# Graph attention on one Trainium2 core: exact float32r passes move from the last projection to the first, and five blocks of W2 are read from DRAM each round

## The chip, the cores and the metric

The kernel runs on one core of a Trainium2 chip. The metric is the device time of one execution in microseconds, the median of several runs. The output must agree with a float32 reference. Engines are named as the profile names them: PE is TensorE (PEld its weight loads), DVE is VectorE, ACT is ScalarE, POOL is GpSimd, SP is SyncE, whose queue issues nearly all DMAs here.

## The reference, cut to what matters

There are 64 graphs of 256 nodes with 512 features. Each goes through a normalisation, a GAT of two attention layers with a residual, a second normalisation, and a third attention layer with a residual.

```python
def gat_layer(x, mask, W, a_src, a_dst, bias, concat):
    xl = (x @ W).reshape(B, N, H, F)
    asrc = jnp.einsum('bnhf,hf->bnh', xl, a_src)
    adst = jnp.einsum('bnhf,hf->bnh', xl, a_dst)
    e = leaky_relu(asrc[:, :, None, :] + adst[:, None, :, :], 0.2)
    attn = softmax(where(mask[..., None], e, NEG_INF), axis=1)
    out = jnp.einsum('bsdh,bshf->bdhf', attn, xl)
    ...
h = maximum(layernorm(x), 0)
h1 = elu(gat_layer(h, mask, W1, ..., concat=True))     # 512 -> 4 heads x 256
x = x + gat_layer(h1, mask, W2, ..., concat=False)     # 1024 -> 1 head x 512
h = maximum(layernorm(x), 0)
x = x + attention(h, adj, W_proj, W_att, b_att)        # 512 -> 8 heads x 64, relu
```

So a graph has three projections: W1 (256x512 by 512x1024), W2 (256x1024 by 1024x512) and W_proj (256x512 by 512x512). Each weight is widened by "logit" columns, W times the attention vectors, so that the scores come out of the same product.

## The kernel before

**Tiles.** A graph's 256 nodes are two tiles (t = 0, 1) of 128 partitions. `Graph` (line 293) has one small method for each step of a graph; `Weights` (line 667) has the steps that prepare weights.

**Three ways of projecting.** The first and second projections are plain float32, as Strassen-Winograd products (`Product`, line 46): a 2x2 split of rows and inner dimension against inner dimension and columns gives seven half-size products instead of eight. Steps `p1` to `p7` are matmuls (line 62), `q1`, `q6`, `q7` copies of a partial sum out of PSUM on ScalarE (line 68), and `q2`, `q3`, `c22`, `q4` write the result (`total`, line 262: a sum on VectorE, or a copy on ScalarE). The left side needs four sums on GpSimd (`left`, line 221), the right side four sums of weight blocks once (`right`, line 626). W1 is done as two column halves `m1a` and `m1b` (tiles `w1a_sb`, `w1b_sb`), W2 as `m2` (`w2_sb`, all seven blocks in SBUF).

The last projection is three float32r passes (lines 524 to 563). The operand is split into a high part (`high3`, ScalarE, times `DOWN`), a low rest (`low3`, GpSimd) and a mixed part (`mix3`, VectorE); the weights are split likewise in `wk_sb`. `u3` and `w3` accumulate two passes in one PSUM bank, `v3` does the third in another; `k3` copies the first out with a factor, `d3` subtracts the second. It works in two halves of 4 heads: 264 columns (4 x 64 features and 2 logits a head) per matmul.

**Turning.** A tile is transposed by writing it to DRAM and reading it back in another layout (`away1`/`home1`, `send2`/`take2`, `away3`/`home3`), then by 32x32 transposes on VectorE (`back1`, `back2`, `back3`). The last graph uses TensorE instead.

**Attention.** `exp`, `ship`, `rows` send the exponentials of the scores over DRAM to all partitions, `edges` (`weigh`, line 286) makes the weights on ScalarE and VectorE, `gat` multiplies on TensorE, `out` divides on VectorE.

**Order.** The order of all instructions is written out by hand as text. `head` runs once, `order` once for each round r = 2 to 62, `tail` at the end. An item such as `-2 m2 p3` is step p3 of the second projection of graph r - 2. A round carries five graphs at different stages. Each engine and SP's DMA queue take their instructions strictly in this order; a DMA whose buffer is not free holds up those behind it. Buffers rotate: `kept` has 3, `hk` 5, `ez` 2.

Of the kernel before, what the change touches and what calls it, by code (L numbers as in the profile page):

```python
# [19 lines left out]
P = 128  # L20
# [12 lines left out]
KEPT = 3  # L33

DOWN = 1.0 - 2.0 ** -13
UP = 1.0 + 2.0 ** -12
LIFT = 2.0 ** 12
EVEN = 2.0 ** -80
# [7 lines left out]
class Product:  # L46
# [8 lines left out]
    def __init__(self, nc, ps_sum, ps_mm, work, lhs, rhs, put):  # L55
        self.nc, self.ps_sum, self.ps_mm, self.work, self.lhs, self.rhs, self.put = (
            nc, ps_sum, ps_mm, work, lhs, rhs, put)
        self.nk, self.n = rhs.shape[2], rhs.shape[3]

    def product(self, to, i, first, last):  # L60
        for c in range(self.nk):
            self.nc.tensor.matmul(to[:, :self.n], self.lhs[:, i, c, :], self.rhs[:, i, c, :],  # L62
                                  start=(first and c == 0), stop=(last and c == self.nk - 1),
                                  skip_group_check=True)

    def kept(self):
        s = self.work.tile([P, 264], F32, name="kept", bufs=KEPT)
        self.nc.scalar.activation(s[:, :self.n], self.sum[:, :self.n], AF.Copy)  # L68
        return s
# [48 lines left out]
def short_path(ctx, tc, flags, x, adj, w1, att_src1, att_dst1, b1, w2, att_src2, att_dst2, b2, w_proj, w_att,  # L118
# [47 lines left out]
    L1, L2 = 4, 1  # L166
    w1_sb = [const.tile([P, 7, DC // 2, L1 + Q], F32, name="w1a_sb"),
             const.tile([P, 7, DC // 2, Q], F32, name="w1b_sb")]
    w2_sb = const.tile([P, 7, HC // 2, L2 + Q], F32, name="w2_sb")
    wk_sb = const.tile([P, 3, 2, DC, G * (K3 + 2)], F32R, name="wk_sb")  # L170
# [97 lines left out]
    def put1(i):  # L268
        at, n = (0, L1 + Q) if i == 0 else (L1, Q)

        def put(t, half, pm, add):
            total(xl1[:, t, 2 * i + half, at:at + n], pm[:, :n], add if add is None else add[:, :n])
        return put

    def put2(t, half, pm, add):
        n = L2 + Q
        total(xl2[:, t, half, :n], pm[:, :n], add if add is None else add[:, :n])

# [14 lines left out]
    class Graph:  # L293


        def __init__(self, b):
# [3 lines left out]
            self.hk, self.us, self.ks, self.vs = {}, {}, {}, {}  # L300
# [54 lines left out]
        def products1(self):  # L355
            self.a1 = work.tile([P, 7, DC // 2, P], F32, name="hs", bufs=1)
            self.m1 = [Product(nc, ps_sum, ps_mm, work, self.a1, w1_sb[i], put1(i)) for i in range(2)]

        def square1(self, t):
            return self.a1[:, 4 * t:4 * t + 2].rearrange("p r k m -> p (r k) m")  # L360

        def turn0(self):
            self.products1()
            for t in range(T):
                turn(self.h, self.square1(t), t)
            left(self.a1, DC // 2)
# [14 lines left out]
        def back1(self, t):  # L381
            if self.a1 == 1:
                self.products1()
            back(self.h, self.square1(t), t)

        def left1(self):
            left(self.a1, DC // 2)
# [7 lines left out]
        def exp1(self):  # L395
            self.exs()
            exps(self.w[0], self.ex1, H1, xl1[:, :, 0, :L1], xl1[:, :, 1, :L1])
# [26 lines left out]
        def ez1(self, g, t):  # L424
            ez = self.e["ez", g, t] = work.tile([P, 2 * F1], F32, name="ez")
# [20 lines left out]
        def back2(self, g, t):  # L446
            if not self.a2:
                self.a2 = work.tile([P, 7, HC // 2, P], F32, name="h1s", bufs=1)
                self.m2 = Product(nc, ps_sum, ps_mm, work, self.a2, w2_sb, put2)
# [3 lines left out]
            else:  # L453
# [3 lines left out]
                nc.scalar.activation(a.rearrange("p k q -> p (k q)"), pm, AF.Copy)  # L457

# [61 lines left out]
        def back3(self, t):  # L520
            self.raw = work.tile([P, DC, P], F32, name="raw", bufs=1)
            (back if self.gone else turn)(self.h, self.raw, t)

        def part(self, i, t):
            a = self.hk[i, t] = work.tile([P, DC, P], F32R, name="hk", bufs=5)
            return a

        def high3(self, t):

            nc.scalar.activation(self.part(0, t), self.raw, AF.Copy, scale=DOWN)  # L530

        def low3(self, t):
            nc.gpsimd.tensor_tensor(self.part(1, t), self.raw, self.hk[0, t].bitcast(F32), ALU.subtract)  # L533

        def mix3(self, t):

            nc.vector.scalar_tensor_tensor(self.part(2, t), self.hk[0, t].bitcast(F32), UP, self.raw, ALU.mult, ALU.subtract)

        def uv(self, pm, i, j, half, t, first, last):
            for c in range(DC):  # L540
                nc.tensor.matmul(pm[:, :G * (K3 + 2)], self.hk[i, t][:, c], wk_sb[:, j, half, c],  # L541
                                 start=(first and c == 0), stop=(last and c == DC - 1))

        def u3(self, half, t):
            self.us[half, t] = ps_sum.tile([P, 512], F32, name="sum")
            self.uv(self.us[half, t], 0, 0, half, t, True, False)

        def w3(self, half, t):
            self.uv(self.us[half, t], 1, 1, half, t, False, True)

        def k3(self, half, t):
            s = self.ks[half, t] = work.tile([P, 264], F32, name="kept", bufs=KEPT)
            nc.scalar.activation(s, self.us.pop((half, t))[:, :264], AF.Copy, scale=UP)

        def v3(self, half, t):
            self.vs[half, t] = ps_mm.tile([P, 512], F32, name="pm")
            self.uv(self.vs[half, t], 2, 2, half, t, True, True)

        def d3(self, half, t):
            def heads(s):  # L560
                return s[:, :G * (K3 + 2)].rearrange("p (h k) -> p h k", h=G)
            nc.vector.tensor_tensor(xl3[:, t, half * G:(half + 1) * G, :K3 + 2], heads(self.ks.pop((half, t))),
                                    heads(self.vs.pop((half, t))), ALU.subtract)
# [47 lines left out]

    graphs = [Graph(b) for b in range(B)]
# [6 lines left out]
    def bring(w, src, at, r, by):  # L619

        nk, n = w.shape[2], w.shape[3]
        for half in range(2):
            rows = src[:, at + half * Q:at + (half + 1) * Q].rearrange("(p c) f -> p c f", p=P)
            by[half].dma_start(blocks(w)[r][half][:, :, n - Q:], rows[:, r * nk:(r + 1) * nk])

    def right(w):
        b11, b21, t2, t1, t3, t4, b22 = (w[:, i] for i in range(7))
# [14 lines left out]
    for r in range(2):  # L642
        bring(w1_sb[1], w1, 2 * Q, r, (nc.sync, nc.scalar))
# [5 lines left out]
    for r in range(2):  # L649
        bring(w1_sb[0], w1, 0, r, (nc.sync, nc.scalar))  # L650
    nc.sync.dma_start(b2_sb, rows_of(b2, D2))
    for a, src in zip(att2, (att_src2, att_dst2)):
        nc.sync.dma_start(a, rows_of(src, D2))
    for r in range(2):
        for half in range(2):
            nc.sync.dma_start(blocks(w2_sb)[r][half][:, :, -Q:],
                              w2[r * (HF // 2):(r + 1) * (HF // 2), half * Q:(half + 1) * Q].rearrange("(p c) f -> p c f", p=P))
        if r == 0:
            nc.sync.dma_start(b1_sb, rows_of(b1, HF))
    nc.sync.dma_start(batt_sb, rows_of(b_att, H3))  # L660
    raw3 = work.tile([P, 2, DC, G * (K3 + 2)], F32, name="h1s", bufs=1)
    for half in range(2):
        for c in range(DC):
            nc.sync.dma_start(raw3[:, half, c].rearrange("p (h k) -> p h k", h=G)[:, :, 2:],
                              w_proj[:, half * Q:(half + 1) * Q].rearrange("(p c) (h k) -> p c h k", p=P, h=G)[:, c])

    class Weights:


        def __init__(self):  # L670

            self.dots = sorted(((r, s, h, c) for s in range(2) for r in range(2) for h in range(H1) for c in range(2)),
                               key=lambda d: (d[2] < 2, d[0] > 0 or d[2] % 2 == 0, d[1]))
            self.sums = {}

        def dots1(self, i):
            for r, s, h, c in self.dots[4 * i:4 * i + 4]:
                dot(blocks(w1_sb[0])[r][s][:, c, h:h + 1], blocks(w1_sb[h // 2])[r][h % 2][:, c, -Q:], att1[s][:, h, :])

        def sums1(self, i):  # L680
            for _ in right(w1_sb[i]):
                pass

        def dots2(self, i):
            r, c = i // 4, i % 4
            for s in range(2):
                for half in range(2):
                    dot(va2[:, i, s, half:half + 1], blocks(w2_sb)[r][half][:, c, -Q:],
                        att2[s][:, half * Q:(half + 1) * Q])

        def columns2(self):
            for r in range(2):
                for s in range(2):
                    v = va2[:, 4 * r:4 * r + 4, s]
                    nc.vector.tensor_tensor(blocks(w2_sb)[r][s][:, :, 0:1], v[:, :, 0:1], v[:, :, 1:2], ALU.add)
            self.sums[2] = right(w2_sb)

        def sums2(self, i):
            next(self.sums[2])

# [4 lines left out]
        def dots3(self, i):  # L705
            c, s = i // 2, i % 2
            for half in range(2):
                blk = raw3[:, half, c].rearrange("p (h k) -> p h k", h=G)
# [5 lines left out]
        def high(self, half):  # L714
            nc.scalar.activation(wk_sb[:, 0, half], raw3[:, half], AF.Copy, scale=DOWN)

        def low(self, half):
            nc.vector.tensor_tensor(wk_sb[:, 1, half], raw3[:, half], wk_sb[:, 0, half].bitcast(F32), ALU.subtract)

        def rest(self, half):  # L720
# [391 lines left out]
```

## Time and profile before

| | |
|---|---|
| time, median of 3 runs | 2964.45 us (2964.36 to 2965.3) |
| the profiled execution: time, span | 2966.22 us, 2964.5 us |
| granted TensorE clock, mean | 0.993 |
| DMA | 513.3 MB, 173 GB/s |

How to read it: a group gives the line, engine, operation, what is written and read, the shape and the count, then busy time in us and the mean duration of one in ns, then the engine's idle time just before them and what ended it. Records of matmuls overlap, so a mean duration is not the time that one adds. In slices of the span each digit is a tenth:

```profile
## 2 busy tenths in 40 slices
PE   5999999999999999999999999999999999999997
PEld 4888888888888888888888888888888888888886
DVE  8888888888888888898888888888888888988886
ACT  3566566566665665665665665656656656656654
POOL 3444444443444444444444444434444444444443
PEclk8999999999999999999999999999999999999999
DMA  5555556656556555555565555555565555555542
```

All slices but the first and the last look alike: these are the rounds. The longest waits of the DMA queue, SP, are for the graph's last sum before its store:

```profile
SPq L610 <- POOL x L603: 402.6, 64, 18.0
SPq L241 <- DVE wt L239: 333.8, 125, 4.1
```

### The profile page before, as it was taken

What the parts mean: (1) busy time and instruction counts of PE and PEld (TensorE: products, weight loads), DVE (VectorE), ACT (ScalarE), POOL (GpSimd) and SP (SyncE); (2) the same over time, 40 slices, a digit from 0 to 9 for tenths busy, and PEclk for the clock granted to TensorE, in tenths of its full rate; (3) what the DMA queues carried; (4) which work ended last, traced back from release to release, by engine and by line L of the source; (5) the groups of instructions that cost most, each with busy time, mean ns of one, the idle gap of its engine ahead of it and who ended that gap; (6) DMA issues with size and microseconds to landing.
All of it is one profiled execution on the core that took longest, in us unless ns stands there. A gap on an engine that the chain in (4) does not pass through costs nothing.

```text
span 2964.5 us, 61553 instructions
## 1 busy us (share of the span) xinstructions
PE 2912.1 (98%) x21576; PEld 2571.5 (87%) x21576; DVE 2602.0 (88%) x6370; ACT 1780.8 (60%) x4557; POOL 1265.4 (43%) x1754
## 2 busy tenths in 40 slices
PE   5999999999999999999999999999999999999997
PEld 4888888888888888888888888888888888888886
DVE  8888888888888888898888888888888888988886
ACT  3566566566665665665665665656656656656654
POOL 3444444443444444444444444434444444444443
PEclk8999999999999999999999999999999999999999
DMA  5555556656556555555565555555565555555542
GB/s 181 161 175 181 174 177 180 176 176 183 174 174 188 174 176 175 175 181 172 175 181 176 171 183 177 178 182 173 176 187 173 177 174 173 182 175 173 181 133 74
DMA packets 540002, 513.30 MB, mean 173 GB/s; under 512 B 89896, under 2 KB 376488, under 8 KB 539688
## 3 DMA queue, kind: packets, MB, share of 16 engines
q1 hardware_dynamic: 538312, 507.20, 56.4%
q8 instruction: 174, 2.85, 0.4%
q10 hardware_dynamic: 1376, 2.10, 0.2%
q14 instruction: 140, 1.15, 0.1%
HBM read 332.01 MB, written 168.79 MB: 169 GB/s over the span
## 4 chain that ended last, share of the span: by engine, by line
PE 95%; DVE 2%; DMA 2%; ACT 0%; issue 0%; POOL 0%; ACTq 0%; SPq 0%; DVEq 0%
PE sum L62 30%; PE pm L62 22%; PE pm L414 15%; PE pm L593 9%; PE sum L541 8%; PE pm L484 7%; PE pm L541 4%; DMA bc<-kept 1%; DVE e L291 0%; DVE o L634 0%; ACT wys L290 0%; DMA kept<-wt 0%; DMA e<-in_L_gnn_att_dst_dram 0%; DMA w1b_sb<-in_L_gnn_W_dram 0%; DMA batt_sb<-in_L_gnn_b_att_dram 0%; DMA xs<-in_x_dram 0%
## 5 line engine op out<-in xcount | busy, mean ns | idle before, releaser
L290 ACT ACTIVATE wys<-bc,exs_sb 128x256 f32<-128x256 f32 x1646 | 715.4, 469 | 157.0 <-DVE e L291 137.7
L414 PE MATMUL pm<-xl,e 128*128 128x257 f32 x2048 | 498.3, 381 | 4.5 <-DVE e L291 3.1
L62 PE MATMUL sum<-w_sb,h1s 128*128 128x257 f32 x2048 | 493.8, 383 | 0.6 <-ACT kept L68 0.6
L291 DVE SCALAR_TENSOR_TENSOR e<-wys,exs_sb,cap 128x256 f32<-128x256 f32 x1024 | 435.8, 467 | 9.8 <-ACT wys L290 8.5
L414 PEld LDWEIGHTS pm<-xl,e 128*128 128x128 f32 x2048 | 380.3, 190 | 56.4 <-DVE e L291 4.6
L62 PEld LDWEIGHTS sum<-w_sb,h1s 128*128 128x128 f32 x2048 | 379.0, 190 | 55.4 <-POOL h1s L227 0.9
L68 ACT ACTIVATE kept<-sum 128x256 f32<-128x256 f32 (+2 forms) x576 | 218.0, 379 | 324.4 <-PE sum L62 323.9
L533 POOL TENSOR_TENSOR hk<-raw,hk 128x512 fp32r<-128x512 f32 x128 | 165.8, 1295 | 489.9 <-ACT exs_sb L284 277.7
L291 DVE SCALAR_TENSOR_TENSOR e<-wys,exs_sb,mask 128x256 f32<-128x256 f32 x640 | 278.7, 477 | 103.0 <-ACT wys L290 102.9
L62 PE MATMUL pm<-w_sb,h1s 128*128 128x257 f32 x1536 | 365.2, 380 | 1.0 <-ACT h1s L457 1.0
L541 PE MATMUL sum<-wk_sb,hk 128*128 128x264 f32 x2048 | 347.0, 302 | 0.0
L62 PEld LDWEIGHTS pm<-w_sb,h1s 128*128 128x128 f32 x1536 | 286.9, 190 | 40.9 <-ACT h1s L457 1.2
L541 PEld LDWEIGHTS sum<-wk_sb,hk 128*128 128x128 f32 x2048 | 287.0, 188 | 11.4 <-ACT hk L530 0.3
L593 PEld LDWEIGHTS pm<-xl,e 128*64 128x64 f32 x8192 | 252.4, 139 | 49.2 <-issue 25.7
L452 DVE STREAM_TRANSPOSE h1s<-z 128x512 f32<-128x512 f32 x252 | 288.1, 1144 | 0.1
L593 PE MATMUL pm<-xl,e 128*64 128x65 f32 x8192 | 271.5, 225 | 5.6 <-DVE e L291 4.8
L62 PE MATMUL sum<-w1b_sb,hs 128*128 128x256 f32 x1024 | 271.4, 388 | 4.1 <-ACT kept L68 2.9
L62 PE MATMUL sum<-w1a_sb,hs 128*128 128x260 f32 x1024 | 269.2, 386 | 6.2 <-DVE w1a_sb L629 3.9
L373 POOL TENSOR_TENSOR x<-x,b_sb 128x512 f32<-128x512 f32 x128 | 166.5, 1302 | 244.3 <-DMA x<-in_x_dram 127.9
L422 DVE SCALAR_TENSOR_TENSOR z<-pm,r,b_sb 128x256 f32<-128x256 f32 x512 | 247.7, 484 | 18.7 <-DVE r L420 0.2
L266 DVE TENSOR_TENSOR xl<-pm,kept 128x256 f32<-128x256 f32 (+2 forms) x576 | 239.0, 415 | 25.3 <-PE pm L62 23.8
L196 POOL TENSOR_SCALAR rstd<-mv 128x2 f32<-128x2 f32 x128 | 28.6, 223 | 514.8 <-DVE mv L192 509.6
(102 smaller groups left out, 5214.8 us busy)
## 6 DMA issues: line engine op xcount, KB each, us to landing
bc<-kept SPq DMA_DIRECT2D x380, 256.0 KB, 3.7
kept_h<-h SPq DMA_DIRECT2D x126, 512.0 KB
h<-kept_h SPq DMA_DIRECT2D x126, 512.0 KB, 4.1
kept_z<-z SPq DMA_DIRECT2D x252, 256.0 KB, 3.9
z<-kept_z SPq DMA_DIRECT2D x252, 256.0 KB, 4.6
xs<-in_x_dram SPq DMA_DIRECT2D x64, 512.0 KB
x<-in_x_dram SPq DMA_DIRECT2D x64, 512.0 KB, 3.5
out_dram<-x SPq DMA_DIRECT2D x64, 512.0 KB
```

The costliest lines, as they stand in the source:

```text
L62: self.nc.tensor.matmul(to[:, :self.n], self.lhs[:, i, c, :], self.rhs[:, i, c, :], start=(first and c == 0), stop=(last and c == self.nk ...
L68: self.nc.scalar.activation(s[:, :self.n], self.sum[:, :self.n], AF.Copy)
L266: nc.vector.tensor_tensor(dst, pm, add, ALU.add)
L290: nc.scalar.activation(wy, bc, AF.Copy, scale=yw)
L291: nc.vector.scalar_tensor_tensor(dst, wy, xw, mask, ALU.max, op)
L373: nc.gpsimd.tensor_tensor(self.x2[:, t], self.x2[:, t], b2_sb, ALU.add)
L414: nc.tensor.matmul(pm[:, :Q + 1], self.e[1, h][:, s, t * P:(t + 1) * P], xl1[:, s, h, L1:], start=(s == 0), stop=(s == T - 1))
L422: nc.vector.scalar_tensor_tensor(self.zt[t][:, sl], pm[:, :Q], r, b1_sb[:, sl], ALU.mult, ALU.add)
L452: nc.vector.transpose(a.rearrange("p k (j q) -> p q k j", q=4), z.rearrange("p (q i c) -> p q c i", q=4, c=4))
L484: nc.tensor.matmul(pm[:, :n], self.e[2][:, s, t * P:(t + 1) * P], xl2[:, s, half, L2:L2 + n], start=(s == 0), stop=(s == T - 1))
L541: nc.tensor.matmul(pm[:, :G * (K3 + 2)], self.hk[i, t][:, c], wk_sb[:, j, half, c], start=(first and c == 0), stop=(last and c == DC - 1))
L593: nc.tensor.matmul(pv[q:q + 64, h, :], self.e[3, a * G + h][:, s, t * P + q:t * P + q + 64], xl3[:, s, a * G + h, 2:], start=(s == 0), sto ...
```

## The change

**First projection.** W1 is no longer done as Strassen-Winograd products but as three float32r passes, in the manner that the last projection had: `high1`, `low1`, `mix1` split the operand, `u1`, `w1`, `v1` multiply, `k1` and `d1` combine. Its 1032 columns (4 heads x 258, of which 2 logits) are taken in three groups of 344: 86 columns out of each head, so a matmul reads four runs of 86. The two logit columns now belong to each head, and all lie in group 0.

**Last projection.** W_proj becomes a Strassen-Winograd product `m3` in plain float32 (`wp_sb`, `hs`), with `left3` and 264 columns.

**W2.** `wk_sb` now holds three splits of all of W1, and only blocks 0 and 3 of W2's seven stay in SBUF. The others are written to DRAM at the start (`keep2`) and read in each round (`bring2`) into two rotating buffers `w2r` of 128 x 4112 bytes: 2 and 1 one round ahead, 4, 5 and 6 in the round that uses them.

**Besides.** `hk` gets 6 buffers, `kept` grows to 344 columns, `ez` has 1 buffer. W1 is loaded into the buffers of `h1s` and `hs`, split there by chunks, and W2 is loaded after it. `head`, `order` and `tail` are written anew.

```diff
+KEPT = 3
+KSZ = 344
+HKS = 6
+W2R = 2
...
-            self.nc.tensor.matmul(to[:, :self.n], self.lhs[:, i, c, :], self.rhs[:, i, c, :],
+            self.nc.tensor.matmul(to[:, :self.n], self.lhs[:, i, c, :], self.rhs(i)[:, c, :],
...
-    L1, L2 = 4, 1
-    w1_sb = [const.tile([P, 7, DC // 2, L1 + Q], F32, name="w1a_sb"),
-             const.tile([P, 7, DC // 2, Q], F32, name="w1b_sb")]
-    w2_sb = const.tile([P, 7, HC // 2, L2 + Q], F32, name="w2_sb")
-    wk_sb = const.tile([P, 3, 2, DC, G * (K3 + 2)], F32R, name="wk_sb")
+    L1, L2, L3 = 2, 1, 2 * G
+    C1 = L1 + Q
+    S1 = C1 // 3
+    wk_sb = const.tile([P, 3, DC, H1, C1], F32R, name="wk_sb")
+    held = (0, 3)
+    w2_sb = const.tile([P, len(held), HC // 2, L2 + Q], F32, name="w2_sb")
+    wp_sb = const.tile([P, 7, DC // 2, L3 + Q], F32, name="wp_sb")
...
+        def back1(self, t):
+            self.raw = work.tile([P, DC, P], F32, name="raw", bufs=1)
+            back(self.h, self.raw, t)
+
+        def part(self, i, t):
+            a = self.hk[i, t] = work.tile([P, DC, P], F32R, name="hk", bufs=HKS)
+            return a
...
+        def some(self, pm, i, j, g, t, first, last):
+            to = pm[:, :H1 * S1].rearrange("p (h f) -> p h f", h=H1)
+            for c in range(DC):
+                nc.tensor.matmul(to, self.hk[i, t][:, c], wk_sb[:, j, c, :, g * S1:(g + 1) * S1],
+                                 start=(first and c == 0), stop=(last and c == DC - 1))
+
+        def u1(self, g, t):
+            self.us[g, t] = ps_sum.tile([P, 512], F32, name="sum")
+            self.some(self.us[g, t], 0, 0, g, t, True, False)
+
+        def w1(self, g, t):
+            self.some(self.us[g, t], 1, 1, g, t, False, True)
+
+        def k1(self, g, t):
+            s = self.ks[g, t] = work.tile([P, KSZ], F32, name="kept", bufs=KEPT)
+            nc.scalar.activation(s, self.us.pop((g, t))[:, :KSZ], AF.Copy, scale=UP)
+
+        def v1(self, g, t):
+            self.vs[g, t] = ps_mm.tile([P, 512], F32, name="pm")
+            self.some(self.vs[g, t], 2, 2, g, t, True, True)
+
+        def d1(self, g, t):
+            def heads(s):
+                return s[:, :KSZ].rearrange("p (h f) -> p h f", h=H1)
+            nc.vector.tensor_tensor(xl1[:, t, :, g * S1:(g + 1) * S1], heads(self.ks.pop((g, t))),
+                                    heads(self.vs.pop((g, t))), ALU.subtract)
...
+        def right2(self, i):
+            return w2_sb[:, held.index(i)] if i in held else self.w2[i]
+
+        def bring2(self, i):
+            self.w2[i] = work.tile([P, HC // 2, L2 + Q], F32, name="w2r", bufs=W2R)
+            nc.sync.dma_start(self.w2[i], kept_w2[i])
...
         def back3(self, t):
+            if self.a3 == 1:
+                self.a3 = work.tile([P, 7, DC // 2, P], F32, name="hs", bufs=1)
+                self.m3 = Product(nc, ps_sum, ps_mm, work, self.a3, lambda i: wp_sb[:, i], DC // 2, L3 + Q, put3)
+            (back if self.gone else turn)(self.h, self.a3[:, 4 * t:4 * t + 2].rearrange("p r k m -> p (r k) m"), t)
...
+            self.dots = [(c, s, h) for c in range(DC) for s in range(2) for h in range(H1)]
...
+        def high(self, c):
+            nc.scalar.activation(wk_sb[:, 0, c, :, L1:], raw(c)[:, :, L1:], AF.Copy, scale=DOWN)
...
+        def logits1(self, c):
+            g, m, r = (wk_sb[:, i, c, :, :L1] for i in range(3))
+            nc.scalar.activation(g, raw(c)[:, :, :L1], AF.Copy, scale=DOWN)
+            nc.vector.tensor_tensor(m, raw(c)[:, :, :L1], g.bitcast(F32), ALU.subtract)
...
+        def keep2(self, i):
+            kept_w2[i] = dram.tile([P, HC // 2, L2 + Q], F32, name=f"kept_w2_{i}", bufs=1)
+            nc.sync.dma_start(kept_w2[i], self.w2[i])
...
     order = """
...
+        0 w1 1 1, 0 k1 1 1, -3 gat3 0 1, -1 back2 0 0, -3 gat3 0 0, -1 back2 1 0, 0 d1 0 1, -1 m2 p1, -1 back2 0 1,
+        1 load, -1 m2 p2, -1 back2 1 1, -2 norm3 1, 0 u1 2 1, -2 norm3 0, 0 exp1, -1 left2, -2 away3, -1 bring2 4,
+        -1 m2 q1, -3 edges3 6, 0 w1 2 1, 0 d1 1 1, 0 ship1, -2 home3, -3 edges3 5, -3 out3 0 1, -1 m2 q2,
+        -3 edges3 4, 0 rows1, 1 stats1 0, -3 out3 0 0, 0 k1 2 1, 1 stats1 1, -3 edges3 7, -1 m2 p5, -2 back3 1,
+        -1 m2 p6, 0 v1 2 0, 0 d1 2 0, -2 back3 0, -2 left3, -1 m2 q6, 0 edges1 1, -1 m2 p7, -3 gat3 1 1, -1 m2 q7,
+        -3 gat3 1 0, -1 m2 c22, -3 out3 1 1, -1 bring2 5, 1 norm1 1, 0 v1 2 1, -2 m3 p1, 0 d1 2 1, 0 edges1 2,
+        -1 m2 p4, 1 norm1 0, 0 gat1 1 0, -1 bring2 6, -3 out3 1 0, 0 cap3, 1 away1, 0 edges1 0, 0 out1 1 0,
+        0 edges1 3, -2 m3 q1, -3 range, -3 store, -1 m2 p3, -1 m2 q3, -1 m2 q4, 0 gat1 0 0, -1 exp2, -2 m3 p6,
...
```

## The prediction

> **What bounds the kernel now.** I read the busy shares first, then busy times by stretch, then TensorE's waits, then the chain, and last the groups of TensorE and VectorE.
>
> From the page, the busy time of each engine:
>
> ```profile
> PE 2912.1 (98%) x21576; PEld 2571.5 (87%) x21576; DVE 2602.0 (88%) x6370; ACT 1780.8 (60%) x4557; POOL 1265.4 (43%) x1754
> ```
>
> From two answers on stretches (TensorE, weight load, VectorE, ScalarE, GpSimd, granted clock, DMA share, GB/s), two of the start and one round in the middle:
>
> ```profile
> 20.00:30.00 10.00, 3.96 (x9) 3.20 (x10) 8.59 (x49) 0.00 (x0) 0.00 (x0) 0.56 1.00 263
> 30.00:40.00 10.00, 6.09 (x15) 4.29 (x14) 9.83 (x41) 0.78 (x2) 0.63 (x1) 0.67 0.36 118
> ...
> 1000.00:1045.05 45.05, 45.05 (x338) 39.94 (x337) 40.03 (x98) 27.69 (x73) 19.57 (x28) 1.00 0.57 177
> ```
>
> Successive stores start 45.05 us apart (59 intervals from 162.3 to 2820.2 us), one graph each. In such a round TensorE is busy without a gap at full clock, VectorE for 40.0 us, and the view of waits cut to 300 to 2700 us lists no wait of TensorE. So a round is the sum of TensorE's instructions. Only at the start is VectorE the bound, while it folds the weights.
>
> Busy records overlap, so the pace is taken from the chain of waits inside that round (start, us, how many instructions):
>
> ```profile
> 1014.36 2.02 PE pm L593 x64
> ...
> 1033.63 1.74 PE pm L62 x8
> 1035.37 0.49 PE pm L541 x4
> 1035.86 1.74 PE pm L62 x8
> 1037.60 0.49 PE sum L541 x4
> 1038.09 0.48 PE pm L541 x4
> ```
>
> A float32 matmul shows as two instructions. One of them over 257 columns takes 1.74/8 = 0.217 us; a float32r matmul is one instruction, and over 264 columns takes 0.484/4 = 0.121 us. Going from one kind to the other costs nothing. Counts and shapes, from the groups with shapes kept apart:
>
> ```profile
> L541 PE MATMUL sum<-wk_sb,hk 128*128 128x264 f32 x2048 | 347.0, 302 | 0.0
> L62 PE MATMUL sum<-w1b_sb,hs 128*128 128x256 f32 x1024 | 271.4, 388 | 4.1 <-ACT kept L68 2.9 <-ACT hs L234 1.1
> L62 PE MATMUL sum<-w1a_sb,hs 128*128 128x260 f32 x1024 | 269.2, 386 | 6.2 <-DVE w1a_sb L629 3.9 <-DVE hs L219 2.1 <-ACT kept L68 0.2
> L62 PE MATMUL pm<-w1a_sb,hs 128*128 128x260 f32 x768 | 201.2, 385 | 8.4 <-DVE w1a_sb L634 8.1 <-DVE r L420 0.4
> L62 PE MATMUL pm<-w1b_sb,hs 128*128 128x256 f32 x768 | 199.8, 383 | 1.3 <-DVE xl L266 1.3
> L541 PE MATMUL pm<-wk_sb,hk 128*128 128x264 f32 x1024 | 175.9, 295 | 0.0
> ```
>
> Divided by 64 graphs: the first projection is 16 + 12 instructions on each of its two halves, the last one 32 + 16.
>
> **What the Trainium skill says.** "FP8 and Floating Point Precision", TensorE Precision Notes: true FP32 is four passes, reduced FP32 reads four bytes and truncates. The pace agrees: two instructions of two sweeps against one of one. "TensorE: Matmul & The Clock Gate", Back-to-back issue gap: N/2.4 + 2.5 ns. For two sweeps of 257 columns that is 216.7 ns (trace 217: agrees); for one of 264 it is 112.5 ns, and the trace has 121: it does not. Same page, LDWEIGHTS: columns/1.2, so 107 ns for 128, overlapped with the running matmul; near enough to 121 to be what paces float32r.
>
> **The change, part by part.**
>
> *TensorE, old.* First projection: 28 x 0.219 (260 columns; chain 0.87 to 0.88 for four) + 28 x 0.216 (256; 0.86) = 12.18 us a graph. Last: 48 x 0.121 = 5.81. Sum 17.99.
>
> *TensorE, new.* First: 3 groups x 2 tiles x 3 passes x 4 chunks = 72 float32r instructions of 344 columns. No row shows this size. Low end: the formula that fits float32, 344/2.4 + 2.5 = 146 ns. High end: in proportion to columns, 121 x 344/264 = 158 ns. What decides is whether 121 ns is a price of the columns or of the weight load. In the tail, transposes of line 456 (128 columns in two sweeps, 107 ns of array) run at 0.48/4 = 0.120 us in the chain at 2894.56. Nearly the same pace at a different column count speaks for a floor of about 120 ns per weight load, which 344 columns clear. Against it: line 259's matmuls, whose weights are one column broadcast, do the same size in 0.112. I take 146: 72 x 0.146 = 10.51 us. The columns are read in four runs of 86; I add nothing for that, up to 0.004 each (0.3 us) if runs cost. Last projection as seven products: 28 x (2 x 264/2.4 + 2.5 = 0.2225) = 6.23. Sum 16.74, so 1.25 us less a round; at 158 ns only 0.38 less. The second projection's matmuls and all attention are the same.
>
> *VectorE.* Removed per graph: 6 sums of about 414 ns and 4 differences of 417 (264 columns). Added: 3 sums of 420, 6 differences of 344 columns. The slope from rows of 264 (417 ns) and 1056 columns (1251) is 1.05 ns a column, so 501 each. 4.15 goes, 4.27 comes: +0.12 us. VectorE then has 40.15 us in a round of 43.8, hidden as long as its remaining 3.6 us of idle time suffice (now 5.0). The mix and the transposes only change graph. *ScalarE*: 12 copies out of PSUM of about 382 ns become 6 of 458 and 4 of 390, slightly less, at 28 of 44 us. *GpSimd*: the two splits and four sums remain as many. ez loses its second buffer: ScalarE waits for VectorE's elu, and has room.
>
> *W2's five blocks.* 128 x 4112 bytes = 526 KB each, 2.63 MB a graph beside the 7.9 now moved (507.2 MB/64), 57% of the engines' time; at the same price a byte +19%, so 76%. Each transfer waits on SyncE's queue for the product that frees its buffer. Blocks 2 and 1 are issued a round ahead: hidden. Blocks 4, 5 and 6 are issued and used within one round. TensorE's work in the new order between the freeing and the using product: block 4 (p2 to p7) 2 x 1.74 + 3 x 0.58 = 5.2 us; block 5 (p6 to p4) 1.74 + 2 x 1.0 + 2 x 0.58 + 0.89 = 5.8; block 6 (p7 to p3) 2.0 + 0.58 + 0.89 + 1.74 + 0.87 = 6.1. The nearest row, 512 KB from DRAM:
>
> ```profile
> x<-in_x_dram SPq DMA_DIRECT2D x64, 512.0 KB, 3.5
> ```
>
> lands in 3.4 to 6.3 us, with 0.4 us of issue before. Usually in time; between 0 and 1.6 us a round may show. I take 0.1, 6 us in all. Ahead of block 4 on SyncE stands the h store of the graph two back, which waits for ScalarE's norm; behind block 4 queue ship1 and rows1, on which the edges of layer 1 wait. If its wait runs long, VectorE is late next.
>
> *The start.* VectorE's weight work: the dots stay, the sums for W1 (6.8 us) go, those for the last projection (4 x 0.70) come, and the split grows from 2 x 2.5 to 4 x 2 x 1.22 plus small columns of 1.6: +2.4 us. Besides, no product of graph 0 can start before all four chunks have their logit columns; about 29 us of VectorE work from 11 us on put that at 40 us. Before, TensorE had 16 us of work in by then, and waited later. I take +10 (0 to 25). *The end*: four GpSimd sums of 0.74 before the last graph's products: +3 (0 to 5).
>
> **Sum.** TensorE is saturated from about 80 to 2880 us, 62 rounds: 62 x 1.25 = -77.5. With +10, +3 and +6 the balance is -58. The profiled execution took 2966.2 us (span 2964.5), the median of the runs is 2964.45, 1.8 less. So 2966.2 - 58.5 - 1.8 = 2906.
>
> **Rivals.**
> 1. *Float32r's price goes with columns* (158 ns): 62 x 0.38 = 24 saved, 19 given back: about 2959; half way, 2935. For it: the formula misses 121 ns. Against: the transposes' equal pace.
> 2. *Blocks come late, and it ends slower.* The place is p7, waiting for block 4 behind a DMA system at three quarters. If it lands in 6.3 us plus 0.4 of issue, p7 waits 1.6 us; 62 x 1.6 = 99, minus the 6 already in: 2999. It decides from a wait of about 1.0 us a round (64/62). For it: the longest landing of the row above. Against: its median.
> 3. *VectorE becomes the bound.* Its 5.0 us of idle time a round are now waits for ScalarE and PSUM; if they do not shrink, a round is 40.15 + 5.0 = 45.15, and with the start and end 2964 + 6 + 13 = 2983. For it: 92% busy. Against: TensorE never waited for it after 300 us.
>
> **How the numbers follow.** Forecast 0.54, rival 1 0.14, rival 2 0.22, rival 3 0.10. Time 2906. The forecast's own range is 2885 to 2945; both signs hold much of the chance, so the 8-in-10 range goes on to the late blocks, 2885 to 3005. Within 0.2% is about what a measurement of this kernel cannot tell from no change. Faster by more: 0.54 and most of rival 1, 0.63; within: 0.05; slower: 0.32.
>
> **What would show it.** Right: stores 43.8 us apart, float32r in the chain at 0.58 us for four, no wait of TensorE in the middle, VectorE 92% busy, first product at about 40 us. Wrong: 0.63 us for four (rival 1); waits of the second projection's products for W2 transfers (rival 2); waits of TensorE for xl or e (rival 3).

## The result, and the profile after

| | before | after |
|---|---|---|
| time, median | 2964.88 us (2964.36 to 2967.53, 4 runs) | 3008.31 us (3005.86 to 3015.88, 4 runs) |
| ratio, with its 95% interval | | 1.0149 (1.013 to 1.0168) |
| span of the profiled execution | 2964.5 us | 3005.8 us |
| first store starts | 168.5 us | 180.7 us |
| 1st to 60th store, 59 rounds | 2656.3 us, 45.02 each | 2689.0 us, 45.58 each |
| from the 60th store to the end | 139.6 us | 136.2 us |

The kernel is 43 us slower; 2906 was predicted, a gain of 58. The last three rows say where to look: of the 41.3 us between the spans, the start has 12.1, the rounds 32.6 and the end -3.5. The start is near what was predicted (+10), the end 6 us better (+3). The rounds are not: each was to become 1.15 us shorter (1.25 saved, 0.1 given back) and has become 0.55 us longer, so 1.7 us a round have to be explained, about 105 us over the 62 rounds of the prediction. Stores are taken here at their issue on SyncE's queue, in both kernels; the 45.05 quoted in the prediction is the same round of the kernel before, read from other edges of the stores.

From the page of the kernel after, the busy shares and the DMA line of the 40 slices:

```profile
PE 2923.4 (97%) x21320; PEld 2594.7 (86%) x21320; DVE 2625.7 (87%) x6314; ACT 1801.6 (60%) x4441; POOL 1306.5 (43%) x1754
...
DMA  6787887877777877877877778788778778777762
```

TensorE has 256 instructions fewer than before and 11 us more of busy time: no saving is in sight. The DMA digits rise from 5 or 6 to 7 or 8. The answers on stretches (the same columns as in the prediction) show the start and the whole middle:

```profile
30.00:40.00 10.00, 3.29 (x11) 2.52 (x10) 9.86 (x24) 6.48 (x10) 2.04 (x3) 1.00 0.66 226
40.00:50.00 10.00, 9.45 (x48) 8.97 (x47) 9.70 (x54) 3.89 (x13) 1.64 (x4) 1.00 0.21 55
...
300.00:2700.00 2400.00, 2386.71 (x17467) 2122.20 (x17462) 2125.04 (x5057) 1468.60 (x3633) 1064.28 (x1423) 1.00 0.79 233
```

TensorE works steadily from about 38 us on, close to the 40 predicted. In the middle the kernel before had TensorE busy for all of the 2400.00 us, at a DMA share of 0.58; now 13 us are idle, and the share is 0.79 (0.76 was estimated). VectorE's 2125 us of 2400 are 89%, not more than before.

The idle 13 us are a third of the loss at most. The rest must lie in the pace, which the timeline of TensorE gives where float32r steps stand together (start, us, and how many instructions):

```profile
1112.16 2.11 PE L398 MATMUL pm<-wk_sb,hk 128*128 128x344 f32 x12
1114.11 2.10 PE L398 MATMUL sum<-wk_sb,hk 128*128 128x344 f32 x12
1116.04 0.81 PE L398 MATMUL pm<-wk_sb,hk 128*128 128x344 f32 x4
```

Twelve instructions take 1116.04 - 1114.11 = 1.93 us from start to start, 0.161 us each. The prediction took 0.146.

### The profile page after: what moved, and what is told of

It is laid out like the page before. It is cut to its first block, busy times and chain, and to the rows that moved or that the text cites. A ratio compares the mean times of both kernels' runs of the same rounds, so it can differ in the third digit from the quotient of the medians.

```text
span 3005.8 us, 62166 instructions
## 1 busy us (share of the span) xinstructions
PE 2923.4 (97%) x21320; PEld 2594.7 (86%) x21320; DVE 2625.7 (87%) x6314; ACT 1801.6 (60%) x4441; POOL 1306.5 (43%) x1754
## 2 busy tenths in 40 slices
DMA packets 586456, 683.37 MB, mean 227 GB/s; under 512 B 95000, under 2 KB 381592, under 8 KB 586136
## 5 line engine op out<-in xcount | busy, mean ns | idle before, releaser
L294 ACT ACTIVATE wys<-bc,exs_sb 128x256 f32<-128x256 f32 x1646 | 717.7, 468 | 493.1 <-DMA bc<-kept 316.0
L398 PE MATMUL sum<-wk_sb,hk 128*128 128x344 f32 x3072 | 626.2, 342 | 41.4 <-ACT hk L386 14.5
L398 PEld LDWEIGHTS sum<-wk_sb,hk 128*128 128x128 f32 x3072 | 513.2, 189 | 76.7 <-ACT xl L270 27.3
L65 PE MATMUL sum<-w2r,h1s 128*128 128x257 f32 x1536 | 371.1, 383 | 4.3 <-DMA w2r<-kept_w 2.6
L65 PEld LDWEIGHTS sum<-w2r,h1s 128*128 128x128 f32 x1536 | 284.8, 189 | 61.2 <-issue 9.4
L398 PE MATMUL pm<-wk_sb,hk 128*128 128x344 f32 x1536 | 309.7, 337 | 1.7 <-DVE hk L393 1.4
L485 DVE STREAM_TRANSPOSE h1s<-z 128x512 f32<-128x512 f32 x252 | 274.9, 1142 | 7.2 <-DMA z<-kept_z 6.8
L65 PE MATMUL sum<-wp_sb,hs 128*128 128x264 f32 x1024 | 271.2, 387 | 1.6 <-DVE hs L225 1.6
L455 DVE SCALAR_TENSOR_TENSOR z<-pm,r,b_sb 128x256 f32<-128x256 f32 x512 | 247.8, 484 | 19.1 <-DVE r L453 0.3
L398 PEld LDWEIGHTS pm<-wk_sb,hk 128*128 128x128 f32 x1536 | 255.0, 189 | 10.1 <-DVE hk L393 1.7
L65 PE MATMUL pm<-w2r,h1s 128*128 128x257 f32 x1024 | 244.0, 380 | 1.2 <-DMA w2r<-kept_w 0.9
L524 PE MATMUL pm<-xl,e 128*128 128x257 f32 (+1 forms) x1024 | 232.3, 379 | 0.2 <-DVE e L295 0.2
L65 PEld LDWEIGHTS pm<-w2r,h1s 128*128 128x128 f32 x1024 | 193.3, 190 | 32.1 <-POOL x L607 2.0
```

Of the source, the lines that this page charges most:

```text
L294: nc.scalar.activation(wy, bc, AF.Copy, scale=yw)
L398: nc.tensor.matmul(to, self.hk[i, t][:, c], wk_sb[:, j, c, :, g * S1:(g + 1) * S1], start=(first and c == 0), stop=(last and c == DC - 1))
L455: nc.vector.scalar_tensor_tensor(self.zt[t][:, sl], pm[:, :Q], r, b1_sb[:, sl], ALU.mult, ALU.add)
L485: nc.vector.transpose(a.rearrange("p k (j q) -> p q k j", q=4), z.rearrange("p (q i c) -> p q c i", q=4, c=4))
L524: nc.tensor.matmul(pm[:, :n], self.e[2][:, s, t * P:(t + 1) * P], xl2[:, s, half, L2:L2 + n], start=(s == 0), stop=(s == T - 1))
```

## The experiments

Two theories were set against each other. *Price*: a float32r matmul of 344 columns costs more than was taken, by its columns, by its four runs of 86, or both. *Transfers*: the five reads of W2 make TensorE wait, for the blocks themselves or for something that their traffic delays. A third, *VectorE*, was rival 3 of the prediction. All ratios are against the kernel before, with 95% intervals.

### What a float32r matmul costs

`micro_f32r` is a kernel by itself, with batches of 64 matmuls that differ in type, columns and runs, four to an accumulation, the weights changed for each:

```diff
+    for k in range(64):
+        nc.tensor.matmul(pms[k // 4 % 2][:, :344], hr[:, k % 4], wr[:, k % 4, :344], ...)
+    for k in range(64):
+        nc.tensor.matmul(pms[k // 4 % 2][:, :344].rearrange("p (h f) -> p h f", h=4), hr[:, k % 4],
+                         w86[:, k % 4, :, 86:172], ...)
```

> No attention layer is computed: the kernel only runs batches of 64 matmuls on split inputs and writes one tile 64 times. It measures the pace of a float32r matmul against its columns. Theory A (weight-load floor, as predicted, with the four runs of 86 columns costing the rest): 128 and 192 columns stay near 0.12 us, 264 0.121, 344 contiguous 0.146, 344 in four runs 0.161, 512 contiguous 0.216. Theory B (price per column, about 0.46 ns): 128 columns 0.06, 192 0.09, 264 0.121, 344 0.158 contiguous, in two and in four runs alike, 512 0.235.

Its chain of waits, from one execution, has one line for each batch (start, us, line, how many instructions); lines 43, 45, 47 and 53 are float32r of 128, 264, 344 and 512 adjacent columns, line 49 is four runs of 86, line 51 two runs of 172, line 57 is float32 of 128 columns, two instructions each. The granted clock is 1.00 through all of them:

```profile
34.70 7.09 PE pm L43 x64
41.79 7.74 PE pm L45 x64
49.53 10.05 PE pm L47 x64
59.58 10.34 PE pm L49 x64
69.92 10.24 PE pm L51 x64
80.17 14.87 PE pm L53 x64
...
102.17 14.31 PE pm L57 x128
```

Divided by 64: 112 ns for 128 columns, 121 for 264, 157 for 344 adjacent, 161 for 344 in four runs, 232 for 512. From 264 to 512 columns the price is about 0.455 ns a column throughout. A floor is there as well: 128 and 192 columns (line 55, 7.13 us for 64) both take 112 ns, and so do the halves of the float32 matmul of 128 columns (14.31/128). But the floor lies below 264 columns, and does not set their price. So 344 columns cost 121 x 344/264 = 157, and the runs 4 ns more. Two runs of 172 cost nearly as much, 160 ns, so it is not a price for each run. The runs also start elsewhere in their rows than the adjacent columns do; the two were not separated.

`contig` gives the four runs up and keeps all else:

```diff
-                nc.tensor.matmul(to, self.hk[i, t][:, c], wk_sb[:, j, c, :, g * S1:(g + 1) * S1],
+                nc.tensor.matmul(pm[:, :KSZ], self.hk[i, t][:, c],
+                                 wk_sb[:, j, c].rearrange("p h f -> p (h f)")[:, g * KSZ:(g + 1) * KSZ],
```

> The changed kernel with each float32r matmul of the first projection reading 344 adjacent columns in place of four runs of 86 (so the columns of a group are others, and the heads mix). Theory A (runs cost 0.015 us a matmul): 72 x 0.015 = 1.1 us a round, 62 rounds, 67 us less: about 2941. Theory A' (runs cost 0.004): 18 us less, 2990. Theory B (price per column): no change, 3008 within 0.2%, four matmuls in 0.64 us as before.

Measured: 2996.57 us (2994.01 to 3004.14), ratio 1.0109 (1.0091 to 1.0126), 11.7 us less than the kernel after. The runs are a real cost in the kernel too, and a small one: 72 x 0.003 = 0.2 us a round by its timeline (0.158 an instruction), and its rounds are 45.39 us, 0.18 less.

### What the reads of W2 cost

`nodma` reads nothing of W2 in the rounds; the two resident blocks are multiplied in place of the five. `quart` keeps every read, every wait and every buffer, but moves a quarter of the bytes, one chunk of each block, which is used for all four:

```diff
-            return w2_sb[:, held.index(i)] if i in held else self.w2[i]
+            return w2_sb[:, held.index(i) if i in held else i % 2]
...
-            nc.sync.dma_start(self.w2[i], kept_w2[i])
+            pass
```

```diff
-            return w2_sb[:, held.index(i)] if i in held else self.w2[i]
+            return w2_sb[:, held.index(i)] if i in held else self.w2[i][:, 0:1].to_broadcast([P, HC // 2, L2 + Q])
...
-            nc.sync.dma_start(self.w2[i], kept_w2[i])
+            nc.sync.dma_start(self.w2[i][:, 0:1], kept_w2[i][:, 0:1])
```

> The changed kernel without the reads of W2's five blocks: the second projection multiplies the two resident blocks in their place. Same work on every compute engine. Theory T (the transfers make other transfers late, above all the broadcast rows that ScalarE waits for, and with them TensorE): the stalls of about 0.5 us a round go, 62 x 0.5 = 31 us less, about 2977; ScalarE's wait for bc falls from 316 us to under 50. Theory P (the price of float32r alone explains the loss): 3008 within 0.3%.

> The changed kernel with a quarter of the bytes of each of W2's five blocks read (one chunk, used for all four), every transfer, its place and its wait for a buffer kept. Theory T by volume (crowded DMA engines): most of what nodma gains, 2977 to 2985. Theory Q (the number of transfers and their waits on SyncE's queue, not the bytes): 3000 to 3008. Theory P: 3008.

Measured: `nodma` 2972.99 us (2971.3 to 2975.26), ratio 1.0023 (1.0013 to 1.0033); `quart` 2969.64 (2966.46 to 2971.73), ratio 1.0015 (1.0008 to 1.0022). So the reads cost 35 to 39 us, and it is their bytes: with the same number of DMAs and of packets (586456 in both traces), issued at the same places behind the same waits, a quarter of the bytes costs nothing that can be seen. Their rounds are 45.07 and 44.99 us. The middle of `quart`, as above:

```profile
300.00:2700.00 2400.00, 2400.00 (x17726) 2155.15 (x17725) 2153.94 (x5122) 1496.88 (x3677) 1084.52 (x1447) 1.00 0.64 192
```

VectorE does the same work for each graph as in the kernel after, in shorter rounds (90% busy), and TensorE has no idle time. That excludes VectorE as the bound. And without the late transfers the change is still not faster than before: the saving on TensorE is not there.

### Who waits for the bytes

Of TensorE's waits between 300 and 2700 us in the kernel after, those for the W2 blocks themselves add up to only 2.2 us. What costs more is seen when one place of one round is laid beside the same place in `quart`. From the timelines of SyncE's queue, ScalarE and TensorE (start, us; the idle time before, and what ended it, in brackets), the kernel after:

```profile
457.33 0.43 SPq L365 DMA_DIRECT2D x<-in_x_dram  x1
459.13 0.33 SPq L256 DMA_DIRECT2D bc<-kept  x1
459.56 0.86 SPq L497 DMA_DIRECT2D w2r<-kept_w  x2
...
465.37 0.87 ACT L294 ACTIVATE wys<-bc,exs_sb 128x256 f32<-128x256 f32 x2 [2.16 <-DMA bc<-kept]
466.18 0.37 ACT L270 ACTIVATE xl<-sum 128x264 f32<-128x264 f32 x1
...
465.12 1.03 PE L447 MATMUL pm<-xl,e 128*128 128x257 f32 x4
466.60 0.92 PE L398 MATMUL sum<-wk_sb,hk 128*128 128x344 f32 x4 [0.46 <-ACT xl L270]
```

and `quart`:

```profile
460.77 0.86 ACT L294 ACTIVATE wys<-bc,exs_sb 128x256 f32<-128x256 f32 x2
461.57 0.37 ACT L270 ACTIVATE xl<-sum 128x264 f32<-128x264 f32 x1
...
462.77 1.03 PE L447 MATMUL pm<-xl,e 128*128 128x257 f32 x4
463.45 0.99 PE L398 MATMUL sum<-wk_sb,hk 128*128 128x344 f32 x4
```

Read it from below. TensorE's float32r step `u1 1 0` of the next graph takes 1.48 us to follow on `gat1` in the kernel after, and 0.68 in `quart`. It needs a PSUM bank that ScalarE's copy `q4` (L270) empties. In ScalarE's order `edges2` (L294) stands ahead of that copy, and it waits 2.16 us for its broadcast row `bc`. The row was issued at 459.13 and used at 465.37; a read of x of 512 KB is issued ahead of it, and two W2 blocks of 514 KB right behind it (`bring2 2` and `bring2 1`). The packets in the two traces show that the row shares the DMA engines with those blocks: its 128 packets take from 460.75 to 465.04, and packets of the blocks run among them from 462.25 on. In `quart`, where the two blocks are a quarter, the row's packets take from 457.99 to 460.14, and it is there in time. Over all 53 rounds from 300 to 2700 us the row takes 3.8 us on average from its first packet to its last in the kernel after, 2.1 in `quart` and 1.7 in `nodma`. The wait for `bc` is no exception: it comes in 46 of these rounds after, 1.7 us on average, and in 2 in `quart`.

The steps of all rounds between 300 and 2700 us, each taken from its start to the start of the next and averaged, give the whole difference. `gat1` ahead of `u1 1 0` takes 1.09 us after and 0.68 in `quart`, and `u1 1 0` itself 0.77 and 0.83, so this place costs 0.35 us a round. The products of W2 and the steps next to them take 16.41 and 16.21, which is 0.20 more; two thirds of that lie around the products on blocks 5 and 6. The step ahead of p7, where block 4 is first used, takes 0.94 us in both. Together these are 0.55 of the 0.58 us by which the rounds differ. So three fifths of the loss come by way of a row of 128 KB that ScalarE waits for, and a third by the products of W2.

### Moving the wait, and moving the reads

`late` puts `edges2` behind q3 and q4; `late_p7` also moves p7 behind a step of `gat3`, since p7 still waits a little for q6's copy; `late_contig` is `late` with adjacent columns.

```diff
-0 send2 0 0, -1 edges2, -2 m3 q3, -2 m3 q4,
+0 send2 0 0, -2 m3 q3, -2 m3 q4, -1 edges2,
```

```diff
-0 edges1 1, -1 m2 p7, -3 gat3 1 1, -1 m2 q7, -3 gat3 1 0
+0 edges1 1, -3 gat3 1 1, -1 m2 p7, -1 m2 q7, -3 gat3 1 0
```

> The changed kernel with one step moved in each round: edges2 of graph r-1 stands after q3 and q4 of the last projection's product in place of before them, so ScalarE no longer waits for the broadcast row in front of the copy that frees the PSUM bank of u1. Theory T (late rows reach TensorE through that copy): TensorE's stalls at the first float32r step after gat1, 18 us in 2400, go; 53 to 62 rounds x 0.34 = 20 us less, about 2988. Rival (the time only moves to the next thing behind edges2, gat2): no change, 3008.

> As late, and gat3 1 1 stands before p7 in place of after it, so TensorE has a microsecond of work while ScalarE copies the sum that p7 goes on with. Theory: the fixed wait of 0.17 us in each round goes as well, 62 x 0.17 = 11 us less than late, about 2977. Rival: gat3 1 1 waits for its edges instead and nothing is won, or it is slower.

> late and adjacent columns together (other columns in each group, heads mixed). If the two are independent, 12 us (as adjacent columns gave alone) and what late gave add up: about 2976. If adjacent columns only moved TensorE's waits, less.

Measured: 3038.58 us, ratio 1.0246 (1.0225 to 1.0267); 3039.44, 1.0251 (1.0233 to 1.0268); 3036.97, 1.0244 (1.0225 to 1.0264). All three are some 30 us slower than the kernel after, where 2976 to 2988 was expected: a miss. The stall after `gat1` is gone (0.68 us in each of the 104 cases of `late`), and another has come. From TensorE's waits in `late`, 300 to 2700 us (us in total, times, longest):

```profile
PE sum L398 <- ACT kept L410: 12.7, 55, 0.9
```

The next bank is freed by `k1` (L410), which stands behind the same row on ScalarE. The idle time shows only a part of it: the three groups of twelve float32r matmuls that follow take 6.67 us a round from start to start, against 6.01 in the kernel after. The rows come no earlier (ScalarE's waits for `bc` are 304.5 us in all, against 316.0), and moving the wait only moved what it delays. Adjacent columns bring nothing clear of the spread of these runs (-1.6 us in the median, where alone they brought 11.7).

`far` takes the traffic away from the row instead: `again` (the read of x) goes behind `rows2`, and `bring2 2` and `bring2 1` go to the end of the round. `far_ship` also sends `ship1` ahead of `bring2 4`.

```diff
--1 ship2, -1 again, ... -1 rows2, ... 0 bring2 2, ... 0 bring2 1, ... 0 send2 1 0
+-1 ship2, ... -1 rows2, -1 again, ... 0 send2 1 0, 0 bring2 2, 0 bring2 1
```

> The changed kernel with transfers moved on SyncE's queue alone: the second load of x (again) stands behind rows2 instead of ahead of it, and the reads of blocks 2 and 1, which have a round of time, stand at the end of the round instead of right behind rows2. The bytes, the number of transfers and the compute engines' order are the same. Theory S (it is what stands around a broadcast row on the queue that makes it late): ScalarE's wait for the row of edges2, 1.6 us in 42 of 48 rounds, goes, with it TensorE's 0.34 us a round; about 21 us less, 2987. Theory V (volume alone): 3000 to 3008.

> As far, and ship1 stands ahead of the read of block 4 instead of behind it, so that the scores of layer 1 leave before SyncE waits for p2. Theory S: ScalarE's wait for the rows of edges1, 2.9 us in 41 of 48 rounds, falls to 1 us or less; another 5 to 15 us less than far, 2972 to 2982. Rival: VectorE, which must turn the scores earlier, waits for ScalarE's exponentials, and it is no faster than far.

Measured: `far` 3070.67 us, ratio 1.0354 (1.0337 to 1.0371); `far_ship` 3052.27, 1.0295 (1.0278 to 1.0312). Both times are far from what was expected. For the cause of the stall `far` is the clearest test all the same: the row of `edges2` takes 2.8 us from its first packet to its last, it is late in only 12 of 51 rounds, by 0.6 us, and the stall after `gat1` is gone (0.68 us in each of 102 cases), without any change in ScalarE's or TensorE's order. But other reads are late in its place. From its lists of waits, the first two lines for the whole span and the last for 300 to 2700 us:

```profile
ACT wys L294 <- DMA bc<-kept: 240.6, 137, 6.2
DVE h1s L485 <- DMA z<-kept_z: 114.1, 64, 3.0
...
PE pm L65 <- DVE xl L419: 25.3, 32, 1.6
```

VectorE's wait for z, read back for the second projection, was 6.8 us in the kernel after. Behind the transposes of z (L485) stands `d1` (L419) in VectorE's order, and `d1` empties the PSUM bank that p2 needs: the same kind of chain as before, by another engine. The step p1, ahead of p2, takes 2.47 us from start to start, against 1.86 in the kernel after. Besides, TensorE's waits for the blocks themselves rise from 2.2 to 14.6 us, which `far_ship` takes back. So the transfers stand in the way of something in both of the places that were tried.

### Is it the volume alone?

`before_traffic` is the kernel before with five copies of the same size a round, from DRAM to DRAM that nobody uses:

```diff
+            s = dram.tile([P, (HC // 2) * (L2 + Q)], F32, name="scr", bufs=8)
+            nc.sync.dma_start(s, w2.rearrange("(p c) f -> p (c f)", p=P)[:, :(HC // 2) * (L2 + Q)])
```

> The kernel before, with five more transfers a round of 128 x 4112 bytes from DRAM to DRAM that nobody waits for, spread over the round. Theory V (such a volume makes other transfers late whatever the order): 20 to 40 us slower, 2985 to 3005, with ScalarE's waits for bc as in the changed kernel. Theory S (it is the new order that leaves the rows too little time): within 0.3% of before, TensorE without waits in the middle.

Measured: 2972.43 us (2969.18 to 2975.68), ratio 1.0022 (1.0015 to 1.003). At a DMA share of 0.79, as high as in the kernel after, it loses 7 us. From its list of waits:

```profile
POOL x L373 <- DMA x<-in_x_dram: 187.9, 35, 6.4
ACT wys L290 <- DMA bc<-kept: 44.5, 55, 4.0
```

Transfers are late here also, but mostly for GpSimd, which has room (127.9 us of such waits in the kernel before); ScalarE waits 44.5 us for its rows (19.1 before), against 316.0 in the kernel after and 153.0 in `quart`. So this volume alone does not cost 38 us in the old order. That the price is made by what a read delays, and by the slack of the order there, fits this and the traces above. But these copies go to DRAM, nobody waits for them, and they stand in other places than the reads; the new order and the kind of transfer were not separated further.

### What would be left

`far_ship_p7_con` adds to `far_ship` the move of p7 and weights laid out so that the 344 columns of each group, the kernel's own, are adjacent. `bound` has the same two on top of `nodma`: the change with no reads at all, and so with none that could be late.

```diff
-    wk_sb = const.tile([P, 3, DC, H1, C1], F32R, name="wk_sb")
+    wk_sb = const.tile([P, 3, DC, 3, H1, S1], F32R, name="wk_sb")
```

> As far_ship, with gat3 1 1 ahead of p7 and the weights of the first projection laid out so that each group of 344 columns is adjacent (same columns as in the changed kernel). If all the parts add: 11 us less by p7, 12 by the adjacent columns, 3 given back at the start for splitting the weights in three pieces; about 2955 from 2975. If the rest of the order limits it: 2965 to 2975, no faster than before.

> What the design would give without its costs: the changed kernel without the reads of W2's blocks (the two resident ones stand in for the five), gat3 1 1 ahead of p7, and each group's 344 columns adjacent. If float32r's price is 0.455 ns a column as measured alone, a round is 45.07 (without the reads) - 0.22 (the wait at p7) - 72 x 0.0045 = 44.53 us: 62 x 0.54 = 33 us less than 2973, about 2940, or 0.8% faster than before. If the start or another wait limits it, 2955 to 2973. The predicted 2906 would need 0.146 us a matmul and is excluded by the price.

Measured: `far_ship_p7_con` 3060.8 us, ratio 1.0319 (1.0302 to 1.0337), 8.5 slower than `far_ship`, which is not explained in full; `bound` 2968.89 (2966.83 to 2971.67), ratio 1.0012 (1.0006 to 1.0019). The move of p7 parts two `gat3` steps that ran together on 64-wide tiles, and the timelines show what that costs, from start to start: in `bound` the two halves take 1.09 and 1.08 us and p7 between them 1.94, 4.11 in all, where in `nodma` p7 and the 64 instructions together take 1.91 + 2.02 = 3.93. That is 0.18 us a round. With the float32r step ahead of p7 counted in, which no longer waits, it is 5.01 against 4.90: the move loses 0.11 us a round and the adjacent columns win 0.19. `bound` with the two left together was not tried; by these figures it would be some 7 us faster (an estimate, 62 x 0.11), and so about 0.1% faster than the kernel before. As measured, without any reads and with adjacent columns, the change comes to the time of the kernel before and not below it. No version that does the whole computation is faster than the kernel before.

## Why the prediction was wrong

**What bounds the kernel.** Right: before, a round is the sum of TensorE's instructions. The first failure is a term of that sum, the second a wait that it left out.

**The step that failed first: "I take 146".** The price of a float32r matmul of 344 columns was to be 146 ns and is 161: 72 x 0.015 = 1.08 us a round, 67 us in 62 rounds. Two terms of it were mis-sized. The column price was taken from a formula that fits float32: "TensorE: Matmul & The Clock Gate", Back-to-back issue gap, of the Trainium skill, N/2.4 + 2.5 ns, which the section gives for a matmul on its own; for a stream with weight loads it says that both set the spacing. The prediction saw that it misses 264 columns by 8.5 ns (112.5 against 121), and explained the miss by a floor at the weight load. The floor exists, at 112 ns (that page's LDWEIGHTS section gives columns/1.2 ns, so 107 for 128 columns; the runs have 112), but 264 columns lie above it and cost 0.455 ns each: 157 - 146 = 11 ns. The other 4 ns are the four runs, named as an upper bound and set to nothing. With 161 the old 17.99 us become 72 x 0.161 + 6.23 = 17.82: a saving of 0.17 us a round in the place of 1.25. The nearest row scaled by columns, 158, would have been right but for the runs. The one argument against it was that transposes of 128 columns ran at nearly the same 120 ns. They are another type of instruction, one record each in the trace, which does not show the two sweeps that the prediction took them for; line 259's 0.112, the evidence on the other side, was the floor that `micro_f32r` then measured.

**The step that failed second: "Blocks 2 and 1 are issued a round ahead: hidden", and 6 us in all.** For TensorE's products on the blocks the size was half of what came: 0.20 us a round, about 12 us, against 0.1 and 6. What was not priced is what the blocks delay. Blocks 2 and 1 are in time for their own users, and go out beside a row that another engine needs in 4 us (issued at 459.13, waited for from 463.21). That costs 0.35 us a round through ScalarE's order and a PSUM bank. In all the reads cost 35 to 39 us. Rival 2 had the sign, and by luck a time (2999) within 10 us of the result, for its mechanism is another: neither p7 nor block 4 is the place. The queue behind block 4 was named, `ship1` and `rows1`, with VectorE as the one that is late next; it was the sharing of the DMA engines, at another pair of blocks, with ScalarE.

**The sum again.** Of the 1.7 us a round, 1.08 are the price and 0.48 the reads (0.58 between the rounds of the kernel after and of `quart`, less the 0.1 foreseen). The 0.14 that remain stay open in part: 17.82 for 17.99 would make the round of `quart` 44.85, and it is 44.99. They fit p7. Next to the same step elsewhere in the round, p7 starts 0.10 to 0.15 us late, with and without the reads; it waits for q6's copy on ScalarE, with only one float32r step between q6's product and p7. The runs did not isolate it, since the move that took the wait away cost more elsewhere.

**VectorE, start, end.** The differences of 344 columns took 495 ns (501 predicted), the copies out of PSUM 441 (458). Rival 3 is excluded by `nodma` and `quart`. The start came out at +12.1 for +10, the end at -3.5 for +3.

**The chances.** Slower had 0.32, and of that most for late blocks. The two errors were held to be independent rivals, each against an otherwise right forecast. Taken together, 158 with 4 for the runs and a wait of the size of rival 2's lead above 3000, a case that the prediction did not work out; the 3008 measured lies just above its 8-in-10 range, which ended at 3005.

## What to carry to other kernels

Price an instruction by the nearest row of the same type scaled to its size; where a formula misses that row, the miss belongs in the price and not in a story about it. When a transfer is hidden from its own user, ask who else has a transfer on the way at that time, which engine waits for it in order, and whose buffer that engine then frees late. A wait that is moved in the order of one engine can come back at the next buffer, as it did in `late`, as long as its cause, a late transfer here, is still there.

## What the runs showed of the hardware

- With a new weight of 128 columns each time, a float32r matmul costs about 0.455 ns a column from 264 to 512 columns (121, 157 and 232 ns), and 112 ns at 128 and at 192 columns. Each of the two instructions of a float32 matmul takes 0.84 ns a column (217 ns for 257, 289 ns for 344).
- Reading the moving operand of 344 columns in four runs of 86 costs float32r 4 ns a matmul (157 to 161 ns), in two runs of 172 3 ns, and float32 nothing: 128 instructions took 37.02 us in four runs and 37.03 adjacent.
- Parting a block of matmuls on 64-wide tiles by a full-width step cost TensorE 0.18 us (4.11 for 3.93 in `bound` and `nodma`).
- Five reads of 514 KB a round that the products wait for cost 35 to 39 us in one order of the work; five copies of that size that nobody waits for cost 7 us in another, at the same DMA share of 0.79.
- Transfers issued behind a row of 128 KB slow it: from its first packet to its last it took 3.8 us on average with two reads of 514 KB right behind it, 2.1 with reads of a quarter, and 1.7 with none of them (`nodma`).
